# Turning h by way of DRAM and VectorE's 32x32 blocks, and running layer 1 a pair of blocks later, in a four-layer graph network

## The chip, the cores and the metric

The kernel runs on one core of a Trainium2 chip. The metric is the device time of one execution in microseconds (us); a lower number is better. A core has TensorE (PE in the profile, with its weight loads shown apart as PEld), VectorE (DVE), ScalarE (ACT), GpSimd (POOL) and SyncE (SP). Here SyncE only issues DMAs. A suffix q (SPq, ACTq) marks what an engine's instruction queue does apart from computing, such as issuing a DMA. Every engine works through its own instructions in order.

## The reference, cut to what matters

There are 128 graphs of 64 nodes with 512 features, so 8192 tokens, all in float32. Four layers follow one another, each with the same frame:

```python
h = max(layernorm(x), 0);  x = x + layer(h, adj, weights)
# layer 0: w_i = scale * q_i . (sum_j adj_ij k_j);  out = softmax over nodes(w) * (h Wv)
# layer 1: p = adj * exp(q k^T), rows divided by their sum;  out = p v
# layer 2: 8 heads, softmax((q k^T) * scale * 2 adj) v, then the product with Wo
# layer 3: T = adj * exp(leaky_relu(s_j + s_i)), rows divided by their sum
#          out = relu(h W0 + (T h) W1 + (T T h) W2 + biases)
```

Each layer thus multiplies h with one to three matrices of 512x512. TensorE sums over partitions, so for those products it needs h with the features on the partitions, while the layer norm gives h with the tokens on the partitions. Between the two h has to be turned.

## The kernel before

**Tiles.** The tokens are worked on in 32 blocks of T = 256 tokens (four graphs), each held as two halves of 128 tokens on the partitions (TT = 2, P = 128). A 512x512 weight has K = 4 chunks of 128 rows. `hT` is h turned: 128 features on the partitions, 4 chunks, 256 tokens.

**Products.** Each product of a block with a 512x512 matrix is done by Strassen's scheme in Winograd's form (class `Product`): seven products of quarter size instead of eight. `sums` (L212 to L229) forms four sums S1 to S4 of quarters of hT on GpSimd (L224 to L227), and the same sums of each weight are formed once (L83 to L100). `Product.first`, `second` and `late` issue the seven products (L259, or L252 where the result is wanted with features on the partitions); between them ScalarE and VectorE take snapshots of partial results (L288, L289, L297, L301), which the late products wait for. `store`, `store_T` and `add_to` combine the results on ScalarE, VectorE and GpSimd. `side_by_side` interleaves two products and takes a list `between` of three places where other work may be put: after the first half-product, before the first late part, before the second late part.

**Norm and turning.** `norm` (L165 to L188) takes statistics of x on VectorE (L170 to L173), a power on GpSimd (L175), one more VectorE operation (L177), and writes h in two halves on ScalarE (L185). `transposed` (L190 to L202) turns it: for each half four products of 128x128 with the identity on TensorE (L196) into PSUM, then one copy of 128x512 to SBUF, on VectorE for the first half (L201), on ScalarE for the second (L199).

**Order of the work.** Layers 0 and 1 are run together, in a list `steps` (L984) of 64 steps: layer 0 of blocks 0 and 1, layer 1 of blocks 0 and 1, layer 0 of blocks 2 and 3, and so on. In step i, `between` holds `prepare` (the norm of the next step, or of the one after it) and, in the third place, `turned(i + 1)`. The end of layer 0 of a block (its softmax and the addition to x, L575 to L596) is put in the first place of the next step; the end of layer 1 of a block (L628 to L649) runs at the end of the next layer 1 step and stores x to DRAM. Behind an odd block's layer 1 step the neighbour sums of the next two blocks (L525 to L545) are done together. Layer 2 then runs over the blocks (L1149 to L1204): in iteration b the q and k products of block b+1 (`layer2_in`), the turning of block b's attention weights (L746, L750), the norm of block b+2 (`prepare2`), the first half of v of block b+1, the context of block b (L767, into `cT` on VectorE L775 and ScalarE L780), the scores of b+1 (L701), the rest of v, then `turned2(b + 2)`, then the output product of block b (`ab_o`, `dc_o`, with sums `S_c` of cT). Layer 3 (`layer3_step`) does per block the products y2 and y1, the product y0, two applications of T, and the end (L946 to L957); its `stages` turn the h of the block after next.

**Planning.** The code is written against a tile framework. It derives the waits, gives out buffers (a tag has a fixed number, `bufs`), and orders each engine's instructions at build time: among those that its own cost estimates call ready it takes the one that stands first in the program. That order is then fixed on the chip. `tc.issue_after(ins)` adds an edge that keeps what follows behind `ins` on the same engine.

Of the kernel before, what the change touches and what calls it, by code (L numbers as in the profile page):

```python
# [16 lines left out]
K = D // P  # L17
H = 8
# [7 lines left out]
def kernel(ctx: ExitStack, tc: tile.TileContext, a: dict, out: bass.AP):  # L26
# [21 lines left out]

    def tokens(ap):
        return ap.rearrange("(t p) d -> p t d", p=P)  # L50
# [5 lines left out]
    def load_x(b: int, source, stage: int):  # L56
        x = big.tile([P, TT, D], FP, tag="x", name=f"x{stage}_{b}", bufs=5)
        nc.sync.dma_start(x, tokens(source))
        return x

    def load_adjT(b: int, stage: int):
        adjT = med.tile([P, TT, N], FP, tag="adjT", name=f"adjT{stage}_{b}")
        nc.sync.dma_start(adjT, tokens(adjT_d[rows(b), :]))
        return adjT
# [37 lines left out]
    def fetched(name: str, place: int, queue):  # L102
        w = slot(place, name)
        for i in range(2):
            for j in range(2):
                queue.dma_start(
                    w[:, quarters[i][j]],
                    a[name][i * F : (i + 1) * F, j * F : (j + 1) * F].rearrange(
                        "(k p) o -> p k o", p=P
                    ),  # L110
                )
        return w
# [16 lines left out]
    def factor(ap, which: str, layer: int, queue):  # L129

        w = slot({"q": 4, "k": 5}[which], f"{which}_{layer}").rearrange("p s k o -> p (s k o)")
        w = [w[:, k * D : (k + 1) * D] for k in range(7)]
        for k in range(K):
            queue.dma_start(w[k], ap[k * P : (k + 1) * P, :])
        return w

    f0 = [
        factor(a["L0_Wqk"][:, i * D : (i + 1) * D], c, 0, queue)
# [24 lines left out]
    behind_norm = {}  # L163

    def norm(x, name: str):  # L165
# [15 lines left out]
        hs = []  # L181
        for t in range(TT):
            h = med.tile([P, D], FP, tag="h", name=f"h_{name}_{t}", bufs=6)
            hs.append(h)
# [3 lines left out]
        return hs  # L188

    def transposed(hs, name: str):  # L190

        hT = big.tile([P, K, T], FP, tag="hT", name=f"hT_{name}")
        for t, h in enumerate(hs):
            pt = ps_tr.tile([P, K, P], FP, tag="tr", name=f"tr_{name}_{t}")
            for k in range(K):
                nc.tensor.transpose(pt[:, k, :], h[:, k * P : (k + 1) * P], ident)  # L196
            ht = hT[:, :, t * P : (t + 1) * P]
            if t % 2:
                nc.scalar.copy(ht, pt)  # L199
            else:  # L200
                nc.vector.tensor_copy(ht, pt)  # L201
        return hT  # L202

    def norm_T(x, name: str):
        hs = norm(x, name)
        return hs, transposed(hs, name)
# [5 lines left out]
    def sums(hT, name: str, places=("S", "S")):  # L212
# [6 lines left out]
            for s in (  # L219
                med.tile([P, 2, 2, P], FP, tag=tag, name=f"S{i}_{name}", bufs=6 if tag == "S" else 3)  # L220
# [249 lines left out]
    def setup1():  # L470
# [33 lines left out]
        def dots(*sums):  # L504
            for to, x, by in sums:
                junk = med.tile([P, D], FP, tag="e2", name="bias1", bufs=3)
# [10 lines left out]
        nc.sync.dma_start(crow.rearrange("o (k p) -> p (o k)", p=P), cc)  # L517
# [136 lines left out]
    def setup2():  # L654
# [3 lines left out]
        made = bvc, row("L2_bo"), fetched("L2_Wv", 0, nc.sync), fetched("L2_Wo", 1, nc.sync)  # L658
# [28 lines left out]
    def layer2_scores(b: int, adjq, qk):  # L687
# [18 lines left out]
        es = []  # L706
        for o in range(2):

            e = med.tile([P, TT, hq // 2, 2, N], FP, tag="e2", name=f"e2_{b}_{o}", bufs=3)
# [15 lines left out]
            es.append(e)  # L725
# [113 lines left out]
    def layer3_norm(b: int):  # L839
        x, adjT = loaded3.pop(b)  # L840
        return x, adjT, norm(x, f"3_{b}")
# [24 lines left out]
    def layer3_in(b: int, x, adjT, hs, e, sj, made: list):  # L866
# [14 lines left out]
        made.append((x, al, sums(transposed(hs, f"3_{b}"), f"3_{b}")))  # L881
# [102 lines left out]
    steps = [(layer, b0 + i) for b0 in range(0, n_blk, 2) for layer in (0, 1) for i in (0, 1)]  # L984
# [3 lines left out]
    def prepare(i: int):  # L988
# [3 lines left out]
        with ExitStack() as behind_sums:  # L992
            if added[0] and not layer:
                behind_sums.enter_context(tc.issue_after(added[0].ins))
            normed[i] = norm(loaded[b][0], f"{layer}_{b}")

    def second():
        with tc.issue_after(of_m0.ins):
            prepare(1)

# [4 lines left out]
    def turned(i: int):  # L1005
        layer, b = steps[i]
        normed[i] = normed[i], transposed(normed[i], f"{layer}_{b}")
# [7 lines left out]
    def prepare2(b: int):  # L1015
        if b < n_blk:
# [4 lines left out]
            normed2[b] = norm(x, f"2_{b}")  # L1021

    def first2(b: int, of_v):
        with tc.issue_after(of_v.kept.ins):
            prepare2(b)

    def turned2(b: int):
        if b < n_blk:
            normed2[b] = transposed(normed2[b], f"2_{b}")
# [19 lines left out]

    for i, (layer, b) in enumerate(steps):  # L1050
        if i == len(steps) - 2:
            fetch2(0)
        between = [[], [chore], []]
# [8 lines left out]
        if i + 1 < len(steps):  # L1062
            if i + 1 not in normed:
                between[0].append(lambda: prepare(i + 1) if i else second())
            if layer and b % 2:
                between[1].append(lambda: prepare(i + 2))
            between[2].append(lambda: turned(i + 1))
        else:
            fetch2(1)
            between[0].append(lambda: first2(0, of_v))  # L1070
            between[2].append(lambda: turned2(0))
        if layer == 0:
            softmax = layer0(b, *loaded[b], *normed[i], aggs.pop(b, None), between)
            begun = [(0, lambda b=b, softmax=softmax: layer0_end(b, *softmax))]
        else:
            before = []
            if b % 2 and i + 2 < len(steps):
                before.append(lambda _: summed(b + 1, normed[i + 1][0], (ps_sc, ps_mm)))
                before.append(lambda _: summed(b + 2, normed[i + 2], (ps_mm, ps_mm)))
# [11 lines left out]
        if i == len(steps) - 3:  # L1091
# [8 lines left out]
    def layer3_step(b: int, ahead: bool = True):  # L1100
# [36 lines left out]
        [lambda: first2(1, of_v), chore], [ends[n_blk - 1], chore], [lambda: turned2(1)]  # L1137
# [135 lines left out]
```

## Time and profile before

| what | value |
|---|---|
| time, median of 3 runs | 2621.78 us (2621.67 to 2622.1) |
| profiled execution, span from first to last instruction | 2619.5 us |
| PE, PEld, DVE, ACT, POOL busy | 2606.0, 2257.8, 1708.7, 952.2, 1290.2 us |
| layers 0 and 1: four steps (two blocks) | 59.26 us |
| layer 2: one block | 28.63 us |
| layer 3: one block | 21.78 us |
| DMA | 129.78 MB, 103198 packets |

The profile gives a span for the profiled execution; the time of a run also holds what lies around the span, and the median is 2.3 us above the span. The three periods are the distances between repeated groups of TensorE in the trace (for example 100.73, 160.06 and 219.31 us for the neighbour sums). In a line of the profile, `out<-in` names what is written and read, `x` the number of instructions, then follow the busy time in us, the mean of one in ns, and the idle time of the engine just before them with what ended it.

### The profile page before, as it was taken

What the parts mean: (1) busy time and instruction counts of PE and PEld (TensorE: products, weight loads), DVE (VectorE), ACT (ScalarE), POOL (GpSimd) and SP (SyncE); (2) the same over time, 40 slices, a digit from 0 to 9 for tenths busy, and PEclk for the clock granted to TensorE, in tenths of its full rate; (3) what the DMA queues carried; (4) which work ended last, traced back from release to release, by engine and by line L of the source; (5) the groups of instructions that cost most, each with busy time, mean ns of one, the idle gap of its engine ahead of it and who ended that gap; (6) DMA issues with size and microseconds to landing.
All of it is one profiled execution on the core that took longest, in us unless ns stands there. A gap on an engine that the chain in (4) does not pass through costs nothing.

```text
span 2619.5 us, 52776 instructions
## 1 busy us (share of the span) xinstructions
PE 2606.0 (99%) x20752; PEld 2257.8 (86%) x20752; DVE 1708.7 (65%) x4400; ACT 952.2 (36%) x2294; POOL 1290.2 (49%) x1582
## 2 busy tenths in 40 slices
PE   9999999999999999999999999999999999999999
PEld 5888888888888889999999999999888888888887
DVE  5666666666676666566566556656677777777675
ACT  3334343433434343333333333333333333333332
POOL 3443334334343435556655655655575555555554
PEclk9999999999999999999999999999999999999999
DMA  5111111111111122111111111111211111111110
GB/s 175 46 35 35 40 48 35 44 43 35 35 35 35 35 76 87 54 38 40 49 43 40 38 54 38 40 50 42 75 51 52 52 52 52 52 52 52 52 43 33
DMA packets 103198, 129.78 MB, mean 50 GB/s; under 512 B 40870, under 2 KB 50086, under 8 KB 102952
## 3 DMA queue, kind: packets, MB, share of 16 engines
q1 hardware_dynamic: 102376, 125.38, 14.5%
q8 instruction: 163, 2.67, 0.4%
q10 hardware_dynamic: 576, 1.05, 0.1%
q14 instruction: 83, 0.68, 0.1%
HBM read 76.07 MB, written 50.34 MB: 48 GB/s over the span
## 4 chain that ended last, share of the span: by engine, by line
PE 97%; DVE 2%; DMA 0%; ACT 0%; issue 0%; POOL 0%; POOLq 0%; ACTq 0%; DVEq 0%
PE ab_y L259 13%; PE ab_v L259 12%; PE dc_y L259 9%; PE dc_v L259 9%; PE ab_k L252 4%; PE ab_q L252 4%; PE ab_g L252 4%; PE ab_o L259 4%; PE tr L196 4%; PE ab_g L259 4%; PE po L400 3%; PE dc_g L252 3%; PE dc_g L259 3%; PE dc_k L252 3%; PE dc_q L252 3%; PE dc_o L259 3%
## 5 line engine op out<-in xcount | busy, mean ns | idle before, releaser
L175 POOL TENSOR_TENSOR rstd<-ve,neghalf 128x2 f32<-128x2 f32 x128 | 89.5, 699 | 359.5 <-DVE ve L173 356.3
L185 ACT ACTIVATE h<-x,nmr,rstd 128x512 f32<-128x512 f32 x256 | 194.3, 806 | 128.0 <-DVE nmr L177 128.0
L259 PE MATMUL ab_y<-L_Wk,hT 128*128 128x256 f32 x768 | 203.9, 388 | 0.1
L259 PE MATMUL ab_v<-L_Wv,hT 128*128 128x256 f32 x768 | 200.7, 384 | 0.0
L259 PE MATMUL dc_v<-L_Wv,S 128*128 128x256 f32 x768 | 197.3, 379 | 0.0
L259 PE MATMUL ab_y<-L_Wk,S 128*128 128x256 f32 x768 | 197.1, 379 | 0.0
L259 PE MATMUL ab_v<-L_Wv,S 128*128 128x256 f32 x768 | 197.1, 379 | 0.0
L259 PEld LDWEIGHTS ab_y<-L_Wk,hT 128*128 128x128 f32 x768 | 138.0, 190 | 66.7 <-issue 24.3
L259 PE MATMUL dc_y<-L_Wk,S 128*128 128x256 f32 x768 | 192.7, 379 | 0.0
L953 POOL TENSOR_TENSOR tz<-tz,y 128x512 f32<-128x512 f32 x62 | 90.4, 1459 | 171.0 <-ACT tz L951 170.9
L170 DVE BATCH_NORM_STATS2 stats<-x 128x6 f32<-128x512 f32 x256 | 164.5, 678 | 0.5
L259 PEld LDWEIGHTS dc_y<-L_Wk,S 128*128 128x128 f32 x768 | 145.7, 190 | 20.5 <-issue 0.8
L259 PEld LDWEIGHTS ab_y<-L_Wk,S 128*128 128x128 f32 x768 | 145.9, 190 | 19.8
L259 PEld LDWEIGHTS ab_v<-L_Wv,S 128*128 128x128 f32 x768 | 145.9, 190 | 19.8
L259 PEld LDWEIGHTS dc_v<-L_Wv,S 128*128 128x128 f32 x768 | 143.4, 190 | 18.9 <-POOL L_Wv L87 0.8
L259 PEld LDWEIGHTS ab_v<-L_Wv,hT 128*128 128x128 f32 x768 | 135.9, 190 | 15.4
L196 PE MATMUL tr<-ident,h 128*128 128x128 f32 x1024 | 132.7, 273 | 0.0
L954 DVE SCALAR_TENSOR_TENSOR x<-tz,x 128x512 f32<-128x512 f32 x62 | 42.9, 692 | 129.7 <-POOL tz L953 129.7
L196 PEld LDWEIGHTS tr<-ident,h 128*128 128x128 f32 x1024 | 118.0, 141 | 6.9 <-issue 0.5
L224 POOL TENSOR_TENSOR S<-hT 128x256 f32<-128x256 f32 x128 | 100.3, 783 | 30.8 <-ACT hT L199 30.4
L227 POOL TENSOR_TENSOR S<-hT 128x256 f32<-128x256 f32 x128 | 106.8, 835 | 7.2 <-DVE hT L201 7.2
L288 ACT COPY p_y<-ab_y 128x256 f32<-128x256 f32 x96 | 35.7, 372 | 191.0 <-PE ab_y L259 191.0
(258 smaller groups left out, 6487.0 us busy)
## 6 DMA issues: line engine op xcount, KB each, us to landing
x<-x SPq DMA_DIRECT2D x128, 512.0 KB, 3.5
x<-in_x_dram SPq DMA_DIRECT2D x32, 512.0 KB, 3.6
out_dram<-x SPq DMA_DIRECT2D x31, 512.0 KB, 2.8
adjT<-in_adjT_dram SPq DMA_DIRECT2D x64, 64.0 KB, 2.2
adjq<-in_adj_dram SPq DMA_DIRECT2D x64, 64.0 KB, 2.3
L_Wk<-in_L_Wk_dram SPq DMA_DIRECT2D x16, 256.0 KB, 4.9
L_Wv<-in_L_Wv_dram SPq DMA_DIRECT2D x12, 256.0 KB, 5.3
q<-in_L_Wqk_dram ACTq DMA_DIRECT2D x4, 256.0 KB, 4.7
```

The lines of the kernel that those rows point to most:

```text
L170: nc.vector.bn_stats(stats[:, t, :], x[:, t, :])
L175: by_rows = nc.gpsimd.tensor_tensor(rstd, ve, neghalf, ALU.pow)
L185: nc.scalar.activation(h, x[:, t, :], AF.Relu, bias=nmr[:, t : t + 1], scale=rstd[:, t : t + 1])
L196: nc.tensor.transpose(pt[:, k, :], h[:, k * P : (k + 1) * P], ident)
L224: nc.gpsimd.tensor_tensor(S1, A21, A22, ALU.add)
L227: behind[0] = nc.gpsimd.tensor_tensor(S3, A11, A21, ALU.subtract)
L252: nc.tensor.matmul(dst[:, m * P : (m + 1) * P], w[:, place, k, m * P : (m + 1) * P], left[:, k, :], start=key not in self.begun, stop=last ...
L259: nc.tensor.matmul(dst, left[:, k, :], w[:, place, k, :], start=key not in self.begun, stop=last and k == 1, skip_group_check=True,)
L288: kept_p[0] = nc.scalar.copy(self.p1, self.a)
L400: nc.tensor.matmul(ps[t][half[g ^ t]], e[half[g], t, :], us[t][half[g]], start=True, stop=True)
L953: nc.gpsimd.tensor_tensor(tz[t], tz[t], y0[:, t, :], ALU.add)
L954: nc.vector.scalar_tensor_tensor(x[:, t, :], tz[t], 0.0, x[:, t, :], ALU.max, ALU.add)
```

## The change

- `norm` writes each half of h, once ScalarE has made it, to a DRAM tensor of its own (`rows_of_h`, two DMAs of 256 KB on ScalarE's queue), and reads it back on SP's queue with four DMAs of 128 KB. Each fills 32 partitions of a tile `part`: partition i*32+q holds, for each group c of 32 tokens, features i*128 to i*128+127 of token c*32+q.
- `transposed` no longer uses TensorE, PSUM or ScalarE. Two VectorE transposes of 128x512 (the second half of the tokens first) turn the 32x32 blocks of `part` into `hT`. The features then lie on the partitions in another order: chunk k, partition i*32+q is feature i*128 + k*32 + q.
- So that the products agree, the weights are loaded with their rows in that order (`by_blocks`): a quarter of a weight in four DMAs of 32 partitions instead of one, a factor of layer 0 or 1 in four DMAs by partitions instead of four by chunks. `plain` keeps the old form where the operand is not h (the k factor of layer 0, `L2_Wo`).
- The turning of the next step's h stands in the first of the three places of a step instead of the third (except in step 0), the norm of the step two later in the second place.
- Layer 1 of a pair of blocks follows layer 0 of the next pair. Six buffers for x instead of five, five for adjT, four for the sums S instead of six. `part` shares buffers with layer 2's exponentials (which become one tile of both halves, two buffers) or, for layer 2's blocks from 2 on, with x.

```diff
-        hs = []
+        hs = {}
+        rows_of_h = tc.dram_tile([T, D], FP, name=f"h_{name}_rows")
         for t in range(TT):
             h = med.tile([P, D], FP, tag="h", name=f"h_{name}_{t}", bufs=6)
-            hs.append(h)
+            hs[t] = h
             nc.scalar.activation(
                 h, x[:, t, :], AF.Relu, bias=nmr[:, t : t + 1], scale=rstd[:, t : t + 1]
             )
-        return hs
+            nc.scalar.dma_start(rows_of_h[t * P : (t + 1) * P, :], h)
+        pool, tag = home
+        part = pool.tile([P, T // Q, P], FP, tag=tag, name=f"part_{name}", bufs=homes[tag])
+        for i in range(4):
+            nc.sync.dma_start(
+                part[i * Q : (i + 1) * Q],
+                rows_of_h.rearrange("(c q) (i f) -> i q c f", q=Q, i=4)[i],
+            )
+        parted[name] = part
+        return [hs[0], hs[1]]
...
-        for t, h in enumerate(hs):
-            pt = ps_tr.tile([P, K, P], FP, tag="tr", name=f"tr_{name}_{t}")
-            for k in range(K):
-                nc.tensor.transpose(pt[:, k, :], h[:, k * P : (k + 1) * P], ident)
-            ht = hT[:, :, t * P : (t + 1) * P]
-            if t % 2:
-                nc.scalar.copy(ht, pt)
-            else:
-                nc.vector.tensor_copy(ht, pt)
+        part = parted.pop(name)
+        for t in (1, 0):
+            nc.vector.transpose(
+                hT[:, :, t * P : (t + 1) * P].rearrange("p k (g q) -> p g k q", q=Q),
+                part[:, t * 4 : (t + 1) * 4].rearrange("p g (k q) -> p g k q", q=Q),
+            )
...
+                for x in range(4):
+                    queue.dma_start(
+                        to[x * Q : (x + 1) * Q], by_blocks(cols)[x][:, 2 * i : 2 * i + 2]
+                    )
...
-    steps = [(layer, b0 + i) for b0 in range(0, n_blk, 2) for layer in (0, 1) for i in (0, 1)]
+    steps = []
+    for b0 in range(0, n_blk + 2, 2):
+        for layer, b in ((0, b0), (1, b0 - 2)):
+            steps += [(layer, b + i) for i in range(2) if 0 <= b < n_blk]
...
-        if i + 1 < len(steps):
-            if i + 1 not in normed:
-                between[0].append(lambda: prepare(i + 1) if i else second())
-            if layer and b % 2:
-                between[1].append(lambda: prepare(i + 2))
-            between[2].append(lambda: turned(i + 1))
+        if i + 1 < n_steps:
+            between[2 if i == 0 else 0].append(lambda: turned(i + 1))
...
+        if i == 0:
+            between[0].append(second)
+        elif i + 2 < n_steps:
+            between[1].append(lambda: prepare(i + 2))
```

## The prediction

> **What bounds the kernel.** I read the busy shares first, then the chain that ended last, then the groups of the removed products, then three stages by windows, and last one iteration of layer 2 by its timeline. From the page:
>
> ```profile
> PE 2606.0 (99%) x20752; PEld 2257.8 (86%) x20752; DVE 1708.7 (65%) x4400; ACT 952.2 (36%) x2294; POOL 1290.2 (49%) x1582
> ...
> PE 97%; DVE 2%; DMA 0%; ACT 0%; issue 0%; POOL 0%; POOLq 0%; ACTq 0%; DVEq 0%
> ```
>
> TensorE is busy for 2606.0 of 2619.5 us, and nearly the whole chain is TensorE's. 13.5 us are idle, 4.7 of them before the first weights land. So a product taken away shortens the kernel by its own length as long as no wait takes its place, and a new wait on PE costs its full length. The groups that the change removes:
>
> ```profile
> L196 PE MATMUL tr<-ident,h 128*128 128x128 f32 x1024 | 132.7, 273 | 0.0
> ...
> L201 DVE COPY hT<-tr 128x512 f32<-128x512 f32 x128 | 86.9, 679 | 0.0
> ...
> L199 ACT COPY hT<-tr 128x512 f32<-128x512 f32 x128 | 74.4, 581 | 81.4 <-PE tr L196 81.3
> ```
>
> The 273 ns are pipelined and overlap. What eight products of one block take from PE is read from the starts in PE's timeline: 318.62 to the next group at 319.49, 292.04 to 292.91, so 0.87 us. The stages:
>
> ```profile
> 100.00:990.00 890.00, 889.82 (x6431) 770.80 (x6430) 602.59 (x1622) 350.90 (x899) 343.47 (x456) 1.00 0.13 42
> ...
> 1050.00:1850.00 800.00, 800.00 (x8706) 745.33 (x8705) 484.13 (x1147) 289.66 (x727) 467.69 (x567) 1.00 0.13 43
> ...
> 1920.00:2580.00 660.00, 660.00 (x3627) 527.54 (x3626) 458.19 (x1230) 221.76 (x457) 341.70 (x398) 1.00 0.15 50
> ```
>
> The columns after the window are its length and the busy time of PE, PEld, DVE, ACT and POOL, then clock, DMA share and GB/s. PE leaves no gap in any stage, at full clock. The starts of repeated groups give 59.26 us for two blocks of layers 0 and 1 (four steps), 28.63 us for a block of layer 2, 21.78 us for one of layer 3.
>
> **What is removed.** 128 turnings of 0.87 us are 111 us (the chain's own share for L196, 4.2% of 2619.5, says 110): 56 in the 64 steps of layers 0 and 1, 28 in layer 2, 28 in layer 3. If nothing waits, 2621.8 - 111 = 2511 us is the floor. The span is 2.3 us under the median of the runs, and I carry those 2.3 us along.
>
> **VectorE.** Per block it loses one copy (0.68) and gains two transposes of 128x512. No such instruction is in the trace. The nearest row is L170, also one SBUF input of 128x512: 0.68 us. Ends: 0.41 (DVE rows of 128x256, such as L314) and 1.12 (L721, 128x512 with two SBUF inputs beside GpSimd). I take 0.68, so +0.68 a block. Load then: layers 0 and 1, 602.59/890 x 59.26 = 40.1, + 4 x 0.68 = 42.8 in 55.8 us, 77%; layer 2, 17.3 + 0.7 = 18.0 in 27.8, 65%; layer 3, 15.1 + 0.7 = 15.8 in 20.9, 76%. At 1.12 the first becomes 46.3, 83%. It does not become the bound on average, but it is in order, and PE waits for its snapshots (L289) and stores (L312 to L314).
>
> The trace shows 0.87 us for eight TensorE turnings in a full stream. The Trainium skill, "VectorE: DVE Perf Modes", The three transpose paths and Rules for kernel authors, speaks against the change: it sends a 128x128 transpose to TensorE where PSUM will do, and has VectorE at 311 ns for such a tile in 16 bits and in 32x32 blocks only. My estimate from that page, four tiles an instruction, is 1.24 us, which would put layers 0 and 1 at 47.3 of 55.8 us of VectorE, still under PE. No row here shows it.
>
> **ScalarE and the queues.** ScalarE loses 0.58 us a block and gains two DMA issues. Its queue's four issues at the start (L134) took 0.41 to 0.46 each; an issue also waits until the activation that writes its h has ended, for which I add 0.2 in all. So what is queued behind the two activations on ScalarE comes 2 x 0.45 + 0.2 = 1.1 us later, and 0.58 us of copy is gone elsewhere. At 36% busy ScalarE carries that; the place where it counts is named under layer 2. SP gets four reads of 128 KB a block at 0.37 to 0.46 (L58, L106), 1.7 us of its sequencer, behind a wait for the two writes. Behind that wait stand the loads of x and adjT for later blocks and the stores of x1, x2 and out; they are needed a step or more later, and SP's longest waits today (21.7 us at L957) already hold them. Traffic grows from 130 MB by 128 x (0.5 + 0.5) MB, about double; the DMA share of 13 to 15% covers that.
>
> **The round trip.** From the page's DMA list:
>
> ```profile
> x<-x SPq DMA_DIRECT2D x128, 512.0 KB, 3.5
> ...
> adjT<-in_adjT_dram SPq DMA_DIRECT2D x64, 64.0 KB, 2.2
> ...
> out_dram<-x SPq DMA_DIRECT2D x2, 256.0 KB, 2.1
> ```
>
> A write of half an h is 256 KB: 2.1 us (ends 2.0, the least landing of all transfers of x, and 4.7, the longest store of L957). A read of 128 KB lies between the 64 KB and 512 KB rows, 2.2 to 3.6: I take 2.5. Four issues at 0.42 put the last landing 3 x 0.42 + 2.5 = 3.8 us after the first issue. From the last write's issue to a turned half: 2.1 + 3.8 + 0.7 = 6.6 us.
>
> SP's row is 0.37 to 0.46 an issue, so cutting one read into four adds 1.3 us. The Trainium skill, "DMA: Bandwidth & Descriptors", Rules for kernel authors, advises one transfer of 128 partitions over several of disjoint partitions, since all spray over the same 16 engines; one read would take those 1.3 us out of the trip.
>
> *Layers 0 and 1.* The norm of the block two steps on is in the middle of a step (about 7 us in), and its transposes come with the first products of the next. That is 14 us for about 3 (norm) + 2.6 (activations, issues) + 6.6: covered, and the sums on POOL are needed only at the next step's start. The pair's delay costs no work; the second x of a pair must wait for a store, about 9 us into its step, still ahead of its use. What is left is VectorE's order: a step with the softmax end, a norm and the transposes holds some 12 us of its work, and a store that comes later than its cover of 1.4 us stalls PE (2.6 us of products lie between the last product of dc and the next on its bank, and three DVE operations of 0.41 take 1.2 of them). I take 0.12 us a step, 8 us in all (0 to 56).
>
> *Layer 3.* Norm and turning are a step and a half apart, VectorE has 3 us idle (before L954) where they fit. Given back: 0.1 a block, 3 us (0 to 10).
>
> *Layer 2* is where it is tight, because norm and turning are in one iteration:
>
> ```profile
> 1376.25 1.52 ACT L185 ACTIVATE h<-x,nmr,rstd 128x512 f32<-128x512 f32 x2 [0.46 <-DVE nmr L177]
> 1377.67 1.11 ACT L780 ACTIVATE cT<-pc,b2v 128x128 f32<-128x128 f32 x4
> ```
>
> ```profile
> 1378.86 0.72 POOL L224 TENSOR_TENSOR S_c<-cT 128x256 f32<-128x256 f32 x1 [2.85 <-ACT cT L780]
> 1379.54 0.73 POOL L227 TENSOR_TENSOR S_c<-cT 128x256 f32<-128x256 f32 x1
> 1380.23 1.18 POOL L225 TENSOR_TENSOR S_c<-S_c,cT 128x256 f32<-128x256 f32 x1
> ```
>
> ```profile
> 1380.03 1.04 PE L196 MATMUL tr<-ident,h 128*128 128x128 f32 x8
> 1380.90 1.03 PE L259 MATMUL ab_o<-L_Wo,cT 128*128 128x256 f32 x4
> 1381.77 1.03 PE L259 MATMUL ab_o<-L_Wo,S_c 128*128 128x256 f32 x4
> ```
>
> (Start, length, engine, line.) The removed turnings are today's cover for the chain ACT cT, POOL S_c: S_c is ready at 1381.41, its product starts at 1381.77, 0.36 us of slack. The change takes 0.87 of cover and puts 1.1 us of issues between h and cT on ScalarE: the product is wanted at 1380.90 and S_c comes at 1382.5, 1.6 us late. The planner may put the two groups of dc_o (1.73 us, needing only cT and the first S_c) in front, then nothing is late. I take half, 0.85, so layer 2 gains nothing. The other path: counted from the iteration's first product (1386.95), h starts at 17.9, the second write is issued at 20.0, lands at 22.1, the reads at 25.9, one half is turned at 26.6 and S made at 27.3 (L224, 0.72). PE wants it at 28.63 - 0.87 = 27.8, later with the stall. It just fits; with 4.7 and 3.6 it comes at 31, 3.3 us late. So back in layer 2: 27 us (0 to 100).
>
> *The ends.* The first weights come in blocks of 32 partitions, so the first product waits for all four pieces (landings 2.6 to 6.9 us), h of block 0 makes the trip where PE has only the fold to do, and eight weights take 96 more issues of SP (44 us at 0.46, spread): 4 us (0 to 12).
>
> **Sum.** 2621.8 - 111 + 8 + 27 + 3 + 4 = 2553 us.
>
> **The rivals.**
> - *All is hidden* (chance 0.20): the planner reorders layer 2, VectorE keeps up; only the start costs: 2511 + 4 = 2515. For it: slack in three stages. Against it: the 0.36 us above.
> - *VectorE sets the pace in layers 0 and 1* (0.12): transposes near 1.12 and late stores, the 56 us there are lost: 2553 + 48 = 2601.
> - *The trip is late, slower than before* (0.21): the transposes stand in VectorE's order before snapshots and stores; if the part lands after the planned moment, VectorE waits and PE behind it. Price in layer 2: the 3.3 us above, 31 x 3.3 = 102 instead of 27; in layers 0 and 1, a part 2 us late against a cover of 1.4, so 0.6 us a step, 38 instead of 8: 2553 + 75 + 30 = 2658. It decides once the trip is some 2 us over my 6.6 in layer 2 and VectorE waits elsewhere too. For it: the 4.7 us landing among the stores; against: their median of 2.8.
> - *Evens out* within 0.2%, 5 us, which is what a measurement here can tell from no change (0.04).
> - *My forecast*, 2530 to 2590 (0.43).
>
> **Numbers.** Faster 0.43 + 0.20 + 0.12 = 0.75; same 0.04; slower 0.21. The range runs from 2512, the floor, to 2630: it takes in the first two rivals and the evening out and leaves out most of the late case, about 2 in 10 (all upper ends together, 56 + 100 + 10 + 12, would give 2689).
>
> **What would show it.** No row L196 tr of h, PE about 2495 busy; transposes x256 at 0.68; in layer 2 an idle of PE before ab_o with POOL S_c as releaser (0.85 each); layer 3 at 20.9 to 21.0 us a block; layers 0 and 1 at 56 to 57 a pair. I am wrong if DVE waits for a DMA in most steps, or if layer 2's period is near 27.8.

## The result, and the profile after

The changed kernel takes 2752.2 us (median of 4 runs, 2748.2 to 2754.0) against 2621.9 (2621.7 to 2622.4) on the same chip: 1.0495 times as long, 95% interval 1.048 to 1.051. The forecast was 2553. Its profiled execution has a span of 2746.4 us, 126.9 more than before.

The same two lines of the page as before the change:

```profile
PE 2584.7 (94%) x19728; PEld 2194.1 (80%) x19728; DVE 1790.2 (65%) x4528; ACT 898.4 (33%) x2166; POOL 1275.2 (46%) x1582
...
PE 61%; DVE 18%; POOL 7%; issue 6%; DMA 6%; ACT 1%; SPq 1%; DVEq 0%; ACTq 0%; POOLq 0%
```

The 1024 products of L196 are gone (20752 to 19728), yet TensorE is busy only 21 us less, and its idle time has grown from 13.5 to 161.7 us. That the busy time fell so little comes in part from products that are recorded as longer: the 64 of pc (the context in layer 2) as 1.89 us instead of 1.16, others under a lower clock, both shown below. The chain that ended last now runs through VectorE, GpSimd and DMAs for a third of its length. VectorE's busy share has not moved from 65%, but its part of the chain has grown from 2% to 18%.

The new operations cost about what was forecast (0.68 us a transpose, 2.1 and 2.5 us a landing). From the page's groups and its DMA list:

```profile
L224 DVE STREAM_TRANSPOSE hT<-part 128x512 f32<-128x512 f32 x256 | 172.9, 694 | 14.4 <-DMA part<-h_rows 12.9
```

```profile
h_rows<-h ACTq DMA_DIRECT2D x256, 256.0 KB, 2.1
part<-h_rows SPq DMA_DIRECT2D x512, 128.0 KB, 3.0
```

The last column of the first line: VectorE waited 12.9 us in all for a read to land. So the trip through DRAM is not where the time shows. TensorE's waits name other places (total, times, longest):

```profile
PE dc_q L274 <- POOL S L246: 59.3, 30, 2.6
PE pa L422 <- DVE u_v L334: 18.4, 13, 1.7
PE dc_g L281 <- POOL S L246: 17.1, 3, 13.4
PE sc L407 <- DVE r L670: 12.6, 14, 0.9
PE ab_y L281 <- DVE u_y L311: 9.3, 30, 1.1
```

By stages, from the starts of the first products of layer 2 (992.1 before, 1027.7 after) and of layer 3 (its first ab_y, 1909.6 and 2050.8):

| stage | if nothing waited | measured | given back | forecast of that |
|---|---|---|---|---|
| start, to the first steady pair | 0 | +36 | 36 | 4 |
| layers 0 and 1, 16 pairs | -56 | 0 (59.2 us a pair, as before) | 56 | 8 |
| layer 2 | -28 | +105 | 133 | 27 |
| layer 3 | -28 | -14 (21.24 a block for 21.78) | 14 | 3 |

36 + 56 + 133 + 14 = 239 where the forecast had 42 (2619.5 - 112 + 239 = 2746.5, the measured span). From here on a number like "1.83 us for pc" is the time from the start of a tile's products to the start of whatever follows on TensorE, added up over an iteration; a wait ahead of the next group is in it.

### The profile page after: what moved, and what is told of

Same layout as the page of the kernel before. It is cut to its first block, busy times and chain, and to the rows that moved or that the text cites. A ratio compares the mean times of both kernels' runs of the same rounds, so it can differ in the third digit from the quotient of the medians.

```text
span 2746.4 us, 52000 instructions
## 1 busy us (share of the span) xinstructions
PE 2584.7 (94%) x19728; PEld 2194.1 (80%) x19728; DVE 1790.2 (65%) x4528; ACT 898.4 (33%) x2166; POOL 1275.2 (46%) x1582
## 4 chain that ended last, share of the span: by engine, by line
PE 61%; DVE 18%; POOL 7%; issue 6%; DMA 6%; ACT 1%; SPq 1%; DVEq 0%; ACTq 0%; POOLq 0%
PE ab_v L281 8%; PE ab_y L281 8%; PE dc_v L281 6%; PE ab_q L274 5%; DVE hu L876 5%; PE dc_y L281 4%; PE ab_k L274 4%; PE ab_g L281 4%; PE dc_q L274 4%; PE dc_k L274 3%; PE ab_g L274 3%; PE dc_g L281 3%; DVE stats L189 3%; PE dc_g L274 2%; DVE y L940 2%
## 5 line engine op out<-in xcount | busy, mean ns | idle before, releaser
L246 POOL TENSOR_TENSOR S<-hT 128x256 f32<-128x256 f32 x128 | 92.9, 726 | 292.5 <-DVE hT L224 292.5
L224 DVE STREAM_TRANSPOSE hT<-part 128x512 f32<-128x512 f32 x256 | 172.9, 694 | 14.4 <-DMA part<-h_rows 12.9
L337 POOL TENSOR_TENSOR v<-u_v,p_v 128x256 f32<-128x256 f32 x64 | 46.7, 729 | 199.0 <-DVE u_v L334 146.3
L876 DVE SCALAR_TENSOR_TENSOR hu<-h,u 128x512 f32<-128x512 f32 x128 | 136.6, 1117 | 0.0
L274 PE MATMUL dc_q<-S,L_Wq 128*128 128x128 f32 x512 | 73.8, 289 | 59.3 <-POOL S L246 59.3
L311 DVE TENSOR_TENSOR u_q<-ab_q,p_q 128x256 f32<-128x256 f32 x32 | 13.6, 424 | 156.7 <-ACT p_q L310 156.7
```

What stands on the lines that cost most here:

```text
L224: nc.vector.transpose(hT[:, :, t * P : (t + 1) * P].rearrange("p k (g q) -> p g k q", q=Q), part[:, t * 4 : (t + 1) * 4].rearrange("p g (k ...
L246: nc.gpsimd.tensor_tensor(S1, A21, A22, ALU.add)
L274: nc.tensor.matmul(dst[:, m * P : (m + 1) * P], w[:, place, k, m * P : (m + 1) * P], left[:, k, :], start=key not in self.begun, stop=last ...
L311: self.kept = nc.vector.tensor_tensor(self.u2, self.b, self.p1, ALU.add)
L337: nc.gpsimd.tensor_tensor(y[:, 1, F:], self.u3, self.p5, ALU.add)
L876: nc.vector.scalar_tensor_tensor(hu, hs[t], 1.0, us[s], ALU.mult, ALU.mult, accum_out=sij[:, s, t : t + 1],)
```

## Layer 2: GpSimd's order, then an order that fills the trip

One iteration of the changed kernel. Start, length, engine, line; in brackets the idle time before and its releaser. TensorE and GpSimd:

```profile
1593.71 1.89 PE L792 MATMUL pc<-pT,v 64*64 64x64 f32 x64
1597.63 1.16 PE L274 MATMUL dc_q<-S,L_Wq 128*128 128x128 f32 x8 [2.03 <-POOL S L246]
```

```profile
1594.41 2.49 POOL L1183 TENSOR_TENSOR x<-x,L_bo 128x512 f32<-128x512 f32 x2
1596.86 0.72 POOL L246 TENSOR_TENSOR S<-hT 128x256 f32<-128x256 f32 x1
```

ScalarE's writes and SP's reads of the trip in that iteration:

```profile
1585.11 1.03 ACTq L208 DMA_DIRECT2D h_rows<-h  x2
1588.45 1.81 SPq L212 DMA_DIRECT2D part<-h_rows  x4
```

GpSimd and TensorE of the kernel before:

```profile
1383.20 0.72 POOL L224 TENSOR_TENSOR S<-hT 128x256 f32<-128x256 f32 x1
1390.80 2.50 POOL L1153 TENSOR_TENSOR x<-x,L_bo 128x512 f32<-128x512 f32 x2
```

```profile
1398.56 1.06 PE L252 MATMUL dc_k<-S,L_Wk 128*128 128x128 f32 x8
1399.45 1.04 PE L746 MATMUL tr<-ident,e 128*128 128x128 f32 x8
```

VectorE had turned the first half, all that the first S needs, by about 1593.9. But GpSimd first adds L2_bo to x, 2.49 us that nobody waits for, and S comes 2.4 us later than it could. In program order that addition stands ahead of the sums. Before the change S was made at 1383.20, long before the addition at 1390.80, so the order did no harm.

The trip itself was longer than its sum: h starts at 1584.27 and its second write is issued by 1586.14, SP issues the four reads from 1588.45 to 1590.26, and they land about 3 us later. That is 7.1 us from the last write's issue, where 5.9 was forecast. In the order of the changed kernel the turning of e (tr, L771) and the context (pc, L792) now stand ahead of q and k, where before they came behind them; e9 will show that they go back when the trip starts earlier.

The idle time has a second price. The windows of the same iteration, where the column before the last two is the granted clock:

```profile
1597.00:1601.00 4.00, 3.37 (x21) 3.37 (x22) 0.00 (x0) 0.00 (x0) 3.92 (x6) 0.73 0.02 6
1601.00:1605.00 4.00, 4.00 (x32) 4.00 (x32) 0.42 (x1) 1.00 (x3) 1.53 (x3) 0.84 0.00 0
```

After the 2.03 us the clock is at 0.73 and 0.84 for 8 us, and this iteration takes 33.01 us. The one before it, with the same wait, kept 1.00 and took 31.38. Of the 24 iterations from 1115.87 on, 13 take 31.4 us, nine 33.0 and two 34.2 (the clock is at 0.50 over the first 4 us of these two). The Trainium skill ("TensorE: Matmul & The Clock Gate", Part 1) has the clock fall after an idle window of about 3.4 us that runs free of the program. Here a gap of 2 us is enough in some iterations and not in others. That it differs from one iteration to the next fits a window that runs free of the program; that 2 us can be enough does not fit the page's length, and the measurement decides.

**e1: the addition behind the sums** (`bias_in` holds the three lines taken out).

```diff
-        with tc.issue_after(behind[0].ins):
-            for t in range(TT):
-                nc.gpsimd.tensor_tensor(x[:, t, :], x[:, t, :], made2[1], ALU.add)
...
             qk, ops = layer2_in(b + 1, normed2[b + 1], [...])
+            bias_in()
```

> In layer 2 only, GpSimd adds L2_bo to x after the sums S of the next block instead of before them; nothing else moves. Theory A (GpSimd's order): in the changed kernel the 2.49 us of L1183 stand between the transposes and L246 (S), and TensorE waits 59.3 us in 30 steps for S. Then this idle falls below 10, layer 2's period goes from 31.39 to 29.0-29.6 us, and the time from 2752 to 2675-2700. Theory B (the round trip through DRAM itself lands too late): S follows the transposes, which stay where they are, the period stays within 0.5 us of 31.39, the time stays between 2735 and 2755, and VectorE's transposes wait for a DMA.

2675.2 us (ratio to before 1.0205, 1.019 to 1.022), 77 less. The wait for S has fallen to 3.1 us in all, most iterations take 29.29 us (a few 29.7 to 30.0), and the clock stays at 1.00 there. Theory A holds. But 29.29 is more than before the change, with 0.87 us of products less: 1.53 us are still missing. They lie in the order that fills the trip. TensorE in e1:

```profile
1466.12 0.66 PE L771 MATMUL tr<-ident,e 128*128 128x128 f32 x4 [0.24 <-POOL e L760]
1466.71 1.89 PE L792 MATMUL pc<-pT,v 64*64 64x64 f32 x64
```

The turning of e follows at once on GpSimd's quotients, and the context at once on ScalarE's copies of the turned e (0.59 us each, the second from 1466.82), with nothing in between: pc takes 1.83 us instead of 0.98, tr 1.43 instead of 0.88.

**e2: products in layer 2 alone** (`norm` without the trip there, L2_Wq, L2_Wk, L2_Wv loaded plain).

> Layer 2 alone turns h with products with the identity again (its Wq, Wk and Wv lie as in the kernel before), layers 0, 1 and 3 stay as changed. Theory A (layer 2's 105 us are made inside layer 2, by the turning): layer 2 takes 916-925 us from its first q product to layer 3's first, as before, against 1022.0, and the time goes to 2640-2655; a few us more at the start, since the two weights of layer 2 are loaded with 8 issues instead of 32, would give 2625-2640. Theory B (the pair's delay, the changed homes of e2, S and x, or the doubled traffic slow layer 2 too): it keeps more than a third of the loss, 955 us or more, and the time stays above 2680.

2630.9 us (1.0035, 1.002 to 1.005). Layer 2 is back at 28.63 us an iteration and 916.5 us in all; the start is 11 us shorter. So the loss in layer 2 is made there, and the changed buffers have no part in it. The traffic of layer 2's own trip is gone here too; e11 below keeps it and is faster than the kernel before in that layer, so it isn't the cause either.

**e9: the norm at the head of the iteration**, on top of e1.

```diff
-            with tc.issue_after(of_qk[b + 1][1].taken.ins):
-                prepare2(b + 2)
...
-                [], [lambda: chore(1 if b else 2), ...
+                [lambda: prepare2(b + 2)], [lambda: chore(1 if b else 2), ...
```

> As e1, and in layer 2 the norm of the block after the next is put at the head of the iteration, beside the first q and k products, instead of behind the stores of q and k: the trip through DRAM starts some 10 us earlier. Theory A (e1's remaining 1.5 us a block, 29.29 us where 28.63 - 0.87 = 27.76 would be the full gain, are the price of an order that fills the trip with the turning of e and the context, ahead of their copies and quotients): these go back to their old places, the period falls to 27.8-28.3 us, the time to 2628-2645; what stays above 27.8 then is a wait of the output products for S_c, as forecast. Theory B (the trip isn't what makes that order, or VectorE's norm in the new place holds up the stores of q and k): 29 us or more a block, 2665 or more.

2676.4 us (1.0209, 1.020 to 1.022): no gain over e1, theory B by the number, and yet A is half right. pc is at 0.98 and tr at 0.88 again, so the late trip did make that order, and products wait for S_c only once, which my forecast had feared for every block. What came instead is a wait ahead of ab_k, 28.7 us in 27 iterations. VectorE, then ScalarE and TensorE in e9:

```profile
1563.85 3.13 DVE L1049 TENSOR_TENSOR x<-x,L_bv 128x512 f32<-128x512 f32 x2
...
1570.94 0.16 DVE L196 SCALAR_TENSOR_TENSOR nmr<-mv,rstd 128x2 f32<-128x2 f32 x1 [2.03 <-POOL rstd L194]
```

```profile
1571.13 1.52 ACT L205 ACTIVATE h<-x,nmr,rstd 128x512 f32<-128x512 f32 x2 [3.90 <-DVE nmr L196]
1572.56 0.35 ACT L310 COPY p_k<-ab_k 128x256 f32<-128x256 f32 x1
```

```profile
1573.42 0.82 PE L274 MATMUL ab_k<-hT,L_Wk 128*128 128x128 f32 x5 [0.69 <-DVE u_k L311]
```

Two additions with two SBUF inputs ran beside each other: VectorE's took 3.13 us (1.28 in e1), GpSimd's 2.94 (2.50). The Trainium skill ("SBUF — State Buffer", SBUF: two separate sides) has VectorE and GpSimd hold one pair of ports by turns in this case, not share it. That both got longer fits; these lengths alone don't tell turns from sharing. Then VectorE waited 2.03 us for rstd, which GpSimd makes, and which now stood behind that addition and the quotients of e. For both reasons h came late, and on ScalarE it stood ahead of the copy that frees ab_k's bank (its buffer in PSUM, which TensorE writes).

**e11: the addition of L2_bo behind the stores of q and k**, on top of e9.

```diff
-            with tc.issue_after(behind[0].ins):
+            with tc.issue_after((of_qk[b + 1][1].stored if b + 1 < n_blk else behind[0]).ins):
```

> As e9, with GpSimd's addition of L2_bo to x put behind its stores of q and k. In e9 the context and the turning of e were back in their places (dc_q to pc: 0.98 us instead of 1.83, tr 0.88), but 1.26 us a block reappeared before ab_k: VectorE's x+L1_bv took 3.13 us beside GpSimd's x+L2_bo (1.28 in e1), and ScalarE made h ahead of the copy that frees ab_k's bank. Theory A (that collision and its delay of h are what was left): the addition on VectorE is at 1.3-1.6 us again, the idle before ab_k (28.7 us in 27 steps) falls below 8, the period from 29.27 to 27.8-28.3 us, the time to 2628-2650. Theory B (the norm at the head of the iteration holds up u_k on ScalarE and VectorE whatever GpSimd does): 29 us a block, 2665-2680.

2637.7 us (1.0062, 1.005 to 1.008), 28.31 us an iteration; the wait before ab_k is gone. The reason was only in small part the one given. VectorE's addition still takes 2.61 us, now beside GpSimd's quotients, but its wait for rstd is short again:

```profile
1515.93 0.16 DVE L196 SCALAR_TENSOR_TENSOR nmr<-mv,rstd 128x2 f32<-128x2 f32 x1 [0.81 <-POOL rstd L194]
```

Counted from the first q product of the iteration, h starts 1.7 us earlier than in e9 (9.8 us for 11.5): 1.2 of it is GpSimd's queue ahead of rstd, 0.5 the two additions. So the copy follows in time. Layer 2 now takes 905.9 us, 12 less than before the change. Its steps: 1023 (changed), 946 (e1), 906 (e11), 889 if nothing waited.

## Layers 0 and 1: the delay cost as much as the products saved

**e8: the delay alone.** Everything of the change but the trip: h turned by products, weights plain, layer 1 two blocks later, the norms in their new places.

> The changed kernel with the pair's delay of layer 1, the changed homes and numbers of buffers, and the new places of the norms, but h is turned with products in every layer and all weights lie as before: no trip through DRAM. Theory A (the delay itself is free, since the 0.87 us of products in each step cover VectorE's and ScalarE's chains): 2617-2628, and 59.2-59.4 us a pair. Theory B (the delay puts the norms ahead of the store that frees the bank for pa, and that costs its 1.4-2 us a pair with products as well): 60.5 us or more a pair, 2640-2655.

2674.3 us (1.0201, 1.019 to 1.021); 62.0 to 64.2 us a pair, 62.6 on average. That is theory B and more (its range ended at 2655). Theory A falls, and with it the forecast's sentence that the delay costs no work: it costs 53 us, with the granted clock at 1.00. (The changed numbers of buffers are in this kernel too; they were not tried apart from the delay.) Set beside it, the changed kernel's 59.2 us a pair say that the turning by DRAM did win its 3.5 us a pair; the delay took them. The two kernels don't lose in quite the same way: in the changed one all of it is at pa, po and sc (3.4 us), while in e8 VectorE also stands still for loads of x that come late, 85.7 us in 26 waits from 100 to 990 us (none before, 3.4 us in the changed kernel). One pair, time on TensorE by tile (us; the others agree within 0.1, but for 0.1 to 0.5 at ab_g and dc_v):

| tile | before | e8, delay alone | changed | e3 |
|---|---|---|---|---|
| tr | 3.49 | 3.50 | 0 | 0 |
| pa | 1.77 | 2.62 | 3.7 | 2.89 |
| po | 2.00 | 3.31 | 3.03 | 2.02 |
| sc | 2.22 | 2.51 | 2.66 | 2.66 |
| pair | 59.26 | 62.6 | 59.2 | 57.6 |

Most of it is in one place, the end of the odd step of layer 1. VectorE and TensorE of the changed kernel there:

```profile
577.88 1.28 DVE L189 BATCH_NORM_STATS2 stats<-x 128x6 f32<-128x512 f32 x2
...
579.81 0.66 DVE L189 BATCH_NORM_STATS2 stats<-x 128x6 f32<-128x512 f32 x1
580.39 0.41 DVE L334 TENSOR_TENSOR u_v<-ab_v,p_v 128x256 f32<-128x256 f32 x1
```

```profile
580.85 0.65 PE L422 MATMUL pa<-h,am 64*64 64x512 f32 x2 [1.24 <-DVE u_v L334]
...
583.84 1.15 PE L407 MATMUL sc<-hT,gT 128*64 128x64 f32 x32 [0.94 <-DVE r L670]
```

Four BATCH_NORM_STATS2, the statistics for the norms of layer 1 of the coming steps, stand ahead of the store L334 that frees the bank for pa, and of the reciprocals that sc waits for. In the kernel before, none stands there:

```profile
574.44 0.42 DVE L312 TENSOR_TENSOR u_v<-ab_v,p_v 128x256 f32<-128x256 f32 x1 [0.51 <-ACT v L311]
...
576.89 0.17 DVE L644 RECIPROCAL r<-sc 128x1 f32<-128x1 f32 x1 [1.17 <-PE den L637]
```

There layer 1's x was finished only in the step before, and that dependence kept its norm out of this place. The delay made the x ready long before, so nothing kept the norm out.

**e3: the norms of layer 1 behind the last additions** (changed kernel).

```diff
-            if added[0] and not layer:
+            if added[0]:
```

> The norms of layer 1 blocks are ordered behind the last addition of the end of layer 1, as those of layer 0 are; nothing else moves. Theory A (VectorE's order at the end of the odd layer 1 steps: norms of two later blocks stand before the store L334 that frees the bank for pa): the idle 1.4 us before pa and part of the stretch to 7.4 us in each of 16 pairs go, the period of a pair falls from 59.26 to 56.5-58, the time by 20-45 to 2707-2732. Theory B (the layers 0 and 1 are held elsewhere, by h being late or by VectorE's load as a whole): the idle moves to another wait, the period stays within 0.4 us of 59.26, the time within 7 us of 2752.

2730.4 us (1.0411, 1.040 to 1.043), 22 less, 57.6 us a pair: theory A. po is back to normal and the wait for r is gone. What stays at pa is another queue: ScalarE makes h of the later block (two activations, 1.52 us) ahead of the copy of v's first quarter.

**e13: the same edit with products (e8).**

> The delay alone with products everywhere (e8), and the norms of layer 1 ordered behind the last additions (the edit of e3). Theory A (the delay costs 53 us because the norms of layer 1, whose x is now complete long before, are taken ahead of the stores that pa, po and sc wait for): the period falls from 62.0-64.2 us a pair to 59.2-60.7, the time to 2625-2648. Theory B (the delay costs by the loads of x that come late, or by ScalarE's h ahead of its copies): 61.5 us or more, above 2655.

2663.5 us (1.0163, 1.015 to 1.018), 61.6 us a pair. By the numbers this is theory B: only 11 of 53 us come back. po is at 2.01 again, but ab_g takes 14.97 us instead of 14.04 and dc_g 11.10 instead of 10.74: the waits moved into the products of g. TensorE waits there for VectorE (9.8 us for wd, 2.3 us for u_g), and VectorE in turn for the loads of x that theory B had named, in the statistics of a norm with the snapshot u_v behind it:

```profile
623.63 0.69 DVE L189 BATCH_NORM_STATS2 stats<-x 128x6 f32<-128x512 f32 x1 [3.25 <-DMA x<-in_x_dram]
624.24 0.41 DVE L325 TENSOR_TENSOR u_v<-ab_v,p_v 128x256 f32<-128x256 f32 x1
```

These waits add up to 42.4 us of VectorE's time; how much of it reaches TensorE was not tried.

**e15: the delay with the old moments** of norm and turning.

```diff
-            between[1].append(lambda: prepare(i + 2))
+            if i + 1 not in normed: between[0].append(lambda: prepare(i + 1))
+            if layer and b % 2: between[1].append(lambda: prepare(i + 2))
...
-            between[2 if i == 0 else 0].append(lambda: turned(i + 1))
+            between[2].append(lambda: turned(i + 1))
```

> The delay alone with products everywhere (e8), with norm and turning at the moments of the kernel before: a block's norm in the step ahead of its own (the two of layer 0 in the odd step of layer 1), its products with the identity at the end of that step. Only the order of the steps is then changed. Theory A (the new moments cost the 53 us: norms a step earlier meet the stores at the end of the odd layer 1 step): 59.2-59.8 us a pair, 2620-2640. Theory B (the order of the steps costs: layer 1 of a pair comes next to layer 0 of the next pair, so that the ends of both meet): 61 us or more a pair, above 2655.

2714.5 us (1.0356, 1.034 to 1.037), about 65.7 us a pair: theory B, and more of it. With the old moments the order of the steps (and the numbers of buffers) costs 93 us; the new moments had mended part of that. Some of the 93 is the clock: it was 0.97 in this stretch (1.00 in e8), and 0.80 and 0.78 in the two windows of 4 us from 593 on, around and behind the wait shown here. VectorE and TensorE at the same place in e15:

```profile
592.50 0.16 DVE L196 SCALAR_TENSOR_TENSOR nmr<-mv,rstd 128x2 f32<-128x2 f32 x1 [1.56 <-POOL rstd L194]
...
594.57 0.16 DVE L680 RECIPROCAL r<-sc 128x1 f32<-128x1 f32 x1
```

```profile
594.78 1.53 PE L421 MATMUL sc<-hT,gT 128*64 128x64 f32 x32 [3.67 <-DVE r L680]
```

VectorE stands still for GpSimd's rstd, with the 0.16 us reciprocal behind it, and TensorE waits 3.67 us for that. A norm costs its queue more than its busy time: it goes to GpSimd and back, and whatever stands behind the second half waits too.

**e14: no delay, the trip in layers 0 and 3 only.** Layer 0's x comes straight from the input, so its norm can be early without any delay.

> Without the delay of layer 1: h goes by way of DRAM and VectorE in layers 0 and 3, where x is ready long before; in layers 1 and 2, where h hangs on the step before, it is turned with products. The norm of the even block of layer 0 is made a step earlier than in the kernel before. Theory A (the delay was needed only for layer 1, and order without it keeps its covers): from e6's 2607 the 32 turnings of layer 0 take 28 us, less what their cover gave at pa (up to 0.9 in each of 16 pairs) and 3-12 at the start, 2580-2605; pairs at 57.4-58.6 us. Theory B (every turning that goes is given back at pa and at the start): 2607-2625.

2617.5 us (0.9985, 0.998 to 0.999), 10 more than layer 3 alone (e6), 59.0 us a pair. Theory B: of the 1.7 us of products that go from a pair, 1.4 come back at po and den, and the start costs some 12 (layer 2 begins 8.4 us later than in e6, after a gain of 4 in the pairs). Turning early is not enough; where the products had been the cover for VectorE's stores, taking them away shows the stores.

## The start

**e4: layer 2's Wq and Wk later, layer 0's Wq in whole pieces** (its order made by the copy behind the product with the identity).

> Two edits at the start: layer 2's Wq and Wk are fetched in step 8 instead of in the set-up of layer 1, and layer 0's Wq is loaded in four pieces of 128 partitions, with its new order made by the copy behind the product with the identity. Theory A (the issues of 32-partition pieces hold SP's and ScalarE's queues): layer 2's first q product comes 15-30 us earlier than 1028.6, of it 13.4 from the idle before 122.9 us and 5-10 from the first product, which starts near 5 us instead of 14.9; the time is 2720-2737. Theory B (the start is held by the first trip of h and by what TensorE can do, and the issues only move): less than 6 us, 2746-2754.

2730.3 us (1.0415, 1.040 to 1.043), 22 less; layer 2 begins at 1009.1 instead of 1027.7: theory A. What held the start is seen in the changed kernel's queues, ScalarE's and SP's. A timeline row runs from the start of its first issue to the end of its last, so the first three rows hold the time between issues too:

```profile
0.73 10.44 ACTq L146 DMA_DIRECT2D q<-in_L_Wqk_dram  x4
```

```profile
102.87 13.66 SPq L121 DMA_DIRECT2D L_Wk<-in_L_Wk_dram  x16
116.57 7.87 SPq L212 DMA_DIRECT2D part<-h_rows  x12
```

The issues themselves (shortest, median and longest in ns, then first and last start), then what SP waited for in the 13.66 us, and two pieces of the chain that ended last:

```profile
L146 ACTq DMA_DIRECT2D q<-in_L_Wqk_dram x4: 317/366/450, 0.7 to 10.9; - x4
L121 SPq DMA_DIRECT2D L_Wk<-in_L_Wk_dram x64: 311/426/1179, 102.9 to 2040.7; - x64
```

```profile
SPq L121 <- DMA h_rows<-h: 5.7, 3, 2.8
```

```profile
1.17 6.06 DMA k<-in_L_Wqk_dram
7.25 5.24 DMA q<-in_L_Wqk_dram
```

So ScalarE's four issues of 256 KB, in pieces of 32 partitions, took under half a microsecond each, but they are spread over 10.44 us. Two went out at once, the third at 7.25 us, just after a transfer of k had landed (1.17 + 6.06 = 7.23). In e4 and in the kernel before, the same bytes in pieces of 128 partitions took 1.86 us with nothing in between. SP's sixteen of 64 KB are spread over 13.66 us, 5.7 of them in three waits that the profile puts to transfers of h; the reads of h stood behind them, and TensorE was idle for 13.37 us then. The forecast's 0.46 us an issue was about right; that a queue can stand still between two issues was not in it. Why these issues wait for another transfer is not shown.

## Layer 3, and the parts together

**e6: the kernel before with the trip in layer 3 alone.**

> The kernel before, with h turned by way of DRAM and VectorE in layer 3 alone (its weights in the new order); layers 0 to 2 and their order as before. Theory A (in layer 3 the trip has a step and a half and is hidden, and 0.54 of 0.87 us a block are gained whatever the other layers do): 30 steps x 0.54 = 16 us less, less some us for 48 issues of weights instead of 12 in the last iterations of layer 2: 2603-2612. Theory B (layer 3's gain comes from the state that the changed layers leave behind, or the issues of the weights hold SP's queue): 2616 or more.

2607.0 us (0.9943, 0.993 to 0.996): theory A. Layer 3 keeps its gain without the other changes; most of the missing third is the wait of ab_y for VectorE's u_y, 8.6 us in 29 steps.

**e5: layer 2 by products, with the edits of e3 and e4.**

> Layer 2 turns h with products, as in e2; the norms of layer 1 stand behind the last additions, as in e3; layer 0's Wq is loaded in pieces of 128 partitions and layer 2's Wq and Wk in step 8, as in e4. Theory A (the losses are separate and add up): from e2's 2630.9, 21-22 us by e3's edit (57.6 against 59.2 us a pair) and 4-10 by e4's (at the first q product e4 is 7 us ahead of e2) go, 2596-2607, faster than the kernel before by 0.6-1.0%. Theory B (the waits replace each other): above 2614.

2604.2 us (0.9933, 0.992 to 0.995): the losses add up.

**e12: the whole change, mended** (e11, e3 and e4).

> The changed kernel with every edit that helped: h goes by way of DRAM and VectorE in all layers, layer 1 two blocks later; in layer 2 the norm at the head of the iteration and the addition of L2_bo behind the stores of q and k (e11), the norms of layer 1 behind the last additions (e3), the weights of the start as in e4. Theory A (the three losses lie in three stages and add up): from e11's 2637.7 e3's 22 and e4's 22 go, 2590-2602 us, faster than the kernel before by 0.7-1.2%, with 28.3 us a block in layer 2, 57.6 a pair in layers 0 and 1, 21.24 a block in layer 3. Theory B (with the waits of one stage gone the next one's come, through the queues of loads that all share): 2606 or more.

2594.0 us (0.9896, 0.988 to 0.991): 28.31 us a block in layer 2, about 57.6 a pair: theory A. So turning h by way of DRAM and VectorE in all layers is worth 27 us, once no queue has something unneeded ahead of what it feeds.

**e16: pa of the later block behind the end of layer 1.**

> As e12, with the neighbour sums pa of the second later block put behind the end of layer 1's block before (po, den) instead of ahead of it. Theory A (pa waits because its h stands ahead of the copy of v's first quarter on ScalarE, and po, which doesn't need that h, can go first): a pair falls from 57.6 to 56.6-57.1 us, the time from 2594.0 to 2578-2586. Theory B (the banks decide: po and pa both wait for v's stores, and the wait only moves from pa to po or sc): within 4 us of 2594.

2593.3 us (0.9894, 0.988 to 0.991), the same as e12: theory B. pa falls to 1.97 us, po and dc_v rise by 0.5 and 0.8, so the wait only moved.

## Why the prediction was wrong

- **The products' 111 us** were sized right: the tr column above and 0.87 us a block say so. With all mended, 27 us of them are kept.
- **VectorE's transposes** were right at 0.68 (694 ns measured). My estimate from the Trainium skill ("VectorE: DVE Perf Modes", The three transpose paths), 1.24, was far too high for this shape and type. VectorE did not become the bound by load.
- **Layers 0 and 1: "The pair's delay costs no work"** is the first step that failed, 8 us for what measured 56. It counted work and left out order. I had priced late stores (0.12 us a step) but did not ask which dependence kept other work away from those stores, and whether the change removed it.
- **Layer 2: "It just fits"** is the second and largest, 27 for 133. The trip was 1.2 us longer than its sum. Above all I let S follow the transposes at once, and did not list what stood on GpSimd's queue: 2.49 us of L1183, 77 us with the clock. The rest was the order that filled the trip and, with the norm early, GpSimd's addition ahead of rstd (40 us by e9 and e11 together); some 0.55 us a block stay. The 27 us were the price of another stall, S_c before ab_o, and that did not appear (3 waits, 5.3 us in all): with the context ahead of q and k S_c has half an iteration of time, and with the norm at the head (e9, e11) h no longer stands between the context and S_c on ScalarE.
- **The start: 4 for 36.** 96 more issues were counted at 0.46 each, and they took about that (median 0.43 for 64 KB). What had no term was that the queues stood still between issues, with the first product and the reads of h behind them; some 19 of the 36 hang on the two places that e4 mends. The rest of the start was not taken apart.
- **Layer 3: 3 for 14**, a size: 0.31 us a block of ab_y's wait for u_y where I took 0.1, 9.3 of the 14.
- **The rival "the trip is late"** had the sign, and most of the size in layer 2 (102 us given back in its sum, 133 measured), but not the mechanism: VectorE hardly waited for a DMA (12.9 us in all). What it got right is luck.
- One reading was wrong without effect: SP's longest wait in the kernel before was 38.6 us at L649, not 21.7 at L957.

What stays open: why the norm of layer 1, put behind the additions, returns 22 us with the trip and only 11 with products (e3, e13), though the late loads of x in e8 and e13 are a candidate; whether the changed numbers of buffers have a part in the delay's 53 us; the other 17 us of the start; and the last 0.55 us a block before the full gain in layer 2, where ab_o waits 0.2 us an iteration for VectorE's u_o.

## What to carry to other kernels

When a change removes work from the bounding engine, or makes data ready earlier, list for each of the other engines what will then stand ahead of the instruction that the bounding engine waits for; a dependence that is loosened lets unneeded work in there. A transfer that takes longer than its gap can cost more through what is put into the gap in its place than through its own wait. And where one part of a change only makes room for another, like the delay here, measure it alone: it can cost just what the other part wins.

## What the runs showed of the hardware

- DMA issues of 256 KB over 32 partitions took 0.32 to 0.45 us each, no longer than over 128 partitions (0.41 to 0.46), but four of them were spread over 10.44 us where four over 128 partitions took 1.86: the queue stood still between them. The Trainium skill's advice ("DMA: Bandwidth & Descriptors", Rules for kernel authors) against pieces of disjoint partitions points the same way; the four reads of each h were not tried as one.
- TensorE's granted clock fell after a gap of 2 us in 11 of 24 iterations and not in the others; an iteration with the fall (to 0.73) took 33.01 us, one without 31.38.
- VectorE's 32x32 transpose of 128x512 in 32 bits takes 694 ns, about as long as a copy of that shape (679 ns, L201 before).
